# Layer 3's last stage: sixteen scatters spread over the dense steps, and seven more dense steps ahead of the slot experts

## The chip, the core and the metric

The kernel runs on one core of one Trainium2 chip, as one launch. The metric is device time in microseconds (us), lower is better; the number quoted is the median of the runs. The core has five engines that run side by side and meet only through semaphores: TensorE (matmuls, PE in the profile, with PEld its weight loads), VectorE (DVE), ScalarE (ACT), GpSimd (POOL) and SyncE (SP, which only issues transfers). GpSimd also issues transfers here, among them all indirect ones (scatters).

## What is computed

A decoder of four layers on x of 4 batches x 512 tokens x 128 channels. Each layer adds self-attention, cross-attention to a context of 77 rows, and a feed-forward block. Only the end of layer 3 matters here: the last batches of cross-attention, and the mixture of experts behind it:

```python
logits = (X @ gate_w.T).astype(jnp.float32)
scores = jax.nn.sigmoid(logits)
_, idx = jax.lax.top_k(scores + bias[None, :], K)          # K = 4 of E = 32
w = jnp.take_along_axis(scores, idx, axis=-1)
w = w / jnp.clip(jnp.sum(w, axis=-1, keepdims=True), 1e-12, None)
...
pos = jnp.take_along_axis(jnp.cumsum(onehot, axis=0) - 1, eid[:, None], axis=1)[:, 0]
valid = pos < C                                            # C = 128 rows an expert
xe = jnp.zeros((E, C, D), x.dtype).at[eid, posc].add(jnp.where(valid[:, None], Xrep, ...))
h = jax.nn.silu(jnp.einsum('ecd,edi->eci', xe, W1)) * jnp.einsum('ecd,edi->eci', xe, W3)
ye = jnp.einsum('eci,eid->ecd', h, W2)
out = yrows.reshape(-1, K, D).sum(axis=1)
out = out + jax.nn.silu(X @ sw1.T) * (X @ sw3.T) @ sw2.T
```

Each of 2048 tokens goes to four of 32 experts, each expert takes at most 128 rows, in the order of the tokens, and a shared expert sees every token.

## The kernel before

The kernel does this mixture in two ways. Batches 0, 1 and 2 are *routed by slots*: each token's row is scattered to its places in a table `slots` in DRAM (32 experts x 128 places, 130 numbers a place: the row, its weight, and where it came from). The experts then run over the table, and each resulting row is scattered to a table `back`, from which four rows a token are fetched and added. Batch 3, whose places can only be known last, is done *densely*: all 16 pairs of experts and the shared expert run over its 512 tokens, and the routing weights (zero where an expert wasn't chosen) multiply the inner result.

The code is written as Python generators that `weave` (L391) advances against one another; a `yield` ends a step. The order so written is the order of priority for a scheduler, which sets the final order on each engine, except where `tc.manual_schedule(engines=...)` fixes an engine's order as written.

The parts, in the order of the program:

- Cross-attention of layer 3 (`l3_xattn`, L2200 on), 64 steps of lagged phases, woven with `chain5(b)` for b = 0, 1, 2: `route_slots` (L750) chooses experts and places, builds `sent` (the rows with weight and origin) and appends 16 scatters to `self.puts` (L789; 128 rows each). `put(n)` (L795) takes scatters off that list and issues them on GpSimd; `scores` of the cross-attention calls it with 2, in the last batch with 3, after each group. At its end `net.put(len(net.puts))` (L2455) issues whatever is left: the sixteen scatters of batch 2.
- Weights. Six packs of layer 3's experts lie in DRAM as bf16. `load` (L371, the issue at L376) fetches each twice: as f32, a transfer with a cast, issued by GpSimd (for the down-projections of batch 3 and all of the slots), and as bf16 unchanged, issued by SyncE (for batch 3's gate and up). The last three f32 packs and four of the bf16 packs go to memory that the cross-attention frees.
- `shared_rows` (L912), two steps for each of batches 0 to 2: the shared expert, whose result is added to x.
- `norm(3)`, `tokens_in_three` (L718), `route_dense` (L730): batch 3's normalised tokens as three bf16 parts, its routing, and the weights' transpose `w3T`. This is `chain`, one step of it being taken for each 0.3 steps of the work it is woven with.
- `ffn("l3_ffn", (3,), ...)` (L968), called `dense`: 17 steps, one for each pair of experts and the shared expert. A step has six bf16 matmuls (gate and up in three parts each), a silu on ScalarE (L1029) into `h` (five buffers), a product by up on VectorE and one by the weights that `spread3` brings out of `w3T`, and, two steps later, one f32 down-matmul into `acc` (L1037).
- `slot_experts` (L830): `fetch` (L842) loads the table in eight groups of four 128-row pieces, over SyncE; for each group `turn` (four transposes, L847), `inner` (gate and up), `inner_turn` (L871) and `down`, which scales the rows by their weights (`made`, L887 and L888) and issues four scatters to `back` (L890) on GpSimd, 32 in all.
- `returned` (L929): three fetches of 1 MB from `back` (L936), four adds a batch to x on VectorE, and the store. `net.out(3)` adds batch 3's dense result and stores it.

The order of these at the end, with the numbers the change touches:

```python
net.weave(chained(*shared, some(dense, 3)), chain, 0.3)
net.weave(net.slot_experts(at["l3"], ff), some(dense, 7), 4, 1)
with tc.manual_schedule(engines={mybir.EngineType.DVE}):
    back = net.returned(range(3), ff)
    next(back)
    net.weave(dense, back, 0.2, 6)
```

So three dense steps stand ahead of the slot experts, seven are woven into them (one for every four slot steps), and seven follow, with the returned rows' adds behind the sixth.

Of the kernel before, what the change touches and what calls it, by code (L numbers as in the profile page):

```python
# [13 lines left out]
F32 = mybir.dt.float32  # L14
# [277 lines left out]
class Net:  # L292
# [361 lines left out]
    def spread(self, w, group, away, pool):  # L654

        nc = self.nc
        T, E = w.shape[1], w.shape[2]
        wp = pool.tile([P, T, E], F32, name="w_halves", tag="w_halves", bufs=1)
        nc.gpsimd.tensor_copy(
            wp.rearrange("p t (h u) -> p t h u", h=2), w.rearrange("p t (u h) -> p t h u", h=2)  # L660
        )
        yield
        for i, b in enumerate(group):
            t = self.sm((E, S))
            for j in range(TB):
                nc.tensor.transpose(t[:, j * P : j * P + P], wp[:, TB * i + j, :], self.ident)
            wT = pool.tile([E, S], F32, tag="w_turned", name="w_turned", bufs=2)
            self.move(wT, t)
            nc.sync.dma_start(away[b], wT)
            yield  # L670
# [124 lines left out]
    def put(self, n):  # L795

        for _ in range(min(n, len(self.puts))):
            self.puts.pop(0)()

    def alone(self, group, put):  # L800

        self.tc.declare_no_dep(put.ins, group=group, reason="rows of their own")
        self.tc.add_to_no_dep_group(group, put.ins)
# [108 lines left out]
    def shared_rows(self, b, W, pool):  # L912

        nc = self.nc
        H = D // 2
        pg, pu = (self.bank("f", (P, S)) for _ in range(2))
        self.dot(pg[:H], (W["gs0"][:, :H], self.tokens(b)))
        self.dot(pu[:H], (W["us0"][:, :H], self.tokens(b)))
        h = pool.tile([P, S], F32, tag="h", name="h", bufs=5)
        nc.scalar.activation(h[:H], pg[:H], AF.Silu)  # L920
        self.tt(h[:H], h[:H], pu[:H], ALU.mult)
        yield
        ps = self.bank("f", (P, TB, D))
        for j in range(TB):
            self.dot(ps[:, j, :], (h[:H, j * P : j * P + P], W["ds0"][:H]))
        self.add_rows(b, ps)
        yield
# [40 lines left out]
    def ffn(self, stage, group, E, base, pool, spread=None):  # L968

        nc = self.nc
        packs = self.units_of(stage, group)
        blocks = [packs[i : i + 2] for i in range(0, len(packs), 2)]
        away = self.chunks[stage] if not spread else None
        rest = [(b, [int(u) for u in routed]) for blk in blocks for b in group for _, _, routed in blk if routed]
        coming = []

        def chunk():  # L980

            if not rest or spread:
                return
            b, units = rest.pop(0)
            c = pool.tile([P, UNITS, S], F32, tag="c", name="c", bufs=3)
            for h in range(2):
                first = h * E // 2 + units[0]
                src = away[b, first : first + len(units)].rearrange("e s -> (e s)")
                nc.sync.dma_start(
                    c[64 * h : 64 * h + 64, : len(units)].rearrange("p e s -> p (e s)"), src.partition_broadcast(64)  # L990
                )
            coming.append(c)

        y = {b: pool.tile([P, S], F32, tag="y", name="y", bufs=2 * len(group)) for b in group}
        self.sums.update({(stage, b): y[b] for b in group})
        chunk()
        chunk()
        at = base
        for k, blk in enumerate(blocks):
            Ws = [self.pack(at + i, n) for i, (n, _, _) in enumerate(blk)]  # L1000
            names = {W: n for W, (n, _, _) in zip(Ws, blk)}
            at += len(blk)
            ahead = at + len(blocks[k + 1]) - 1 if k + 1 < len(blocks) else at + 1
            for b in group:
                units = [(W, u, None) for W, (_, sh, _) in zip(Ws, blk) for u in sh]
                plan = []
                for W, (_, sh, routed) in zip(Ws, blk):
                    plan += [(W, u, None) for u in sh] + [(W, u, i) for i, u in enumerate(routed)]
                acc, cs = {}, {}
                for i, (W, u, in_c) in enumerate(plan):  # L1010
                    if in_c is not None and spread:
                        if u not in cs:
                            cs.update(spread([v for _, v, in_c in plan[i : i + 2] if in_c is not None]))
                        cu = cs.pop(u)
                    elif in_c is not None:
                        if in_c == 0:
                            chunk()
                            c = coming.pop(0)
                        cu = c[:, in_c, :]
                    pg, up = self.bank("f", (P, S)), self.bank("f", (P, S))  # L1020
                    for ps, w in ((pg, "g"), (up, "u")):
                        if spread:

                            wb = self.in_bf16[names[W]][w + u]
                            self.dot(ps, *[(wb, self.x3[:, i]) for i in range(3)])
                        else:
                            self.dot(ps, (W[w + u], self.tokens(b)))
                    h = pool.tile([P, S], F32, tag="h", name="h", bufs=5)
                    nc.scalar.activation(h, pg, AF.Silu)  # L1029
                    self.tt(h, h, up, ALU.mult)  # L1030
                    if in_c is not None:
                        self.tt(h, h, cu, ALU.mult)

                    def down(W=W, u=u, h=h, i=i, b=b, acc=acc, n=len(plan), k=k):
                        if i == 0:
                            acc["t"] = self.acc()
                        nc.tensor.matmul(acc["t"], lhsT=W["d" + u], rhs=h, start=i == 0, stop=i == n - 1)  # L1037
                        if i == n - 1 and k == 0:
                            nc.scalar.copy(y[b], acc["t"])
                        elif i == n - 1:  # L1040
                            self.tt(y[b], y[b], acc["t"], ALU.add)

                    self.last.append(down)
                    if len(self.last) > 2:
                        self.last.pop(0)()
                    if b == group[0] and i == 2:
                        self.want(ahead)
                    yield
# [1231 lines left out]
def chained(*chains):  # L2280
    for c in chains:
        yield from c


def some(steps, n):

    for _ in range(n):
        if next(steps, steps) is steps:
            return
        yield  # L2290


def build(nc, packs, dram):
# [9 lines left out]
    at = {}  # L2303
# [6 lines left out]
    with tile.TileContext(nc) as tc, ExitStack() as ctx:  # L2310
        net = Net(ctx, tc, packs, dram, feed)
# [3 lines left out]
        def open_pool(name, right=False):  # L2315
            pools[name] = ExitStack()
            return pools[name].enter_context(net.pool(name, right=right))
# [29 lines left out]
        ff = open_pool("ff")  # L2347
# [60 lines left out]
        dense = lambda b: net.l2_dense(b, y[b], w4, s4)  # L2408
# [26 lines left out]
        steps = net.l3_xattn(at["x3"], x3)  # L2435
# [14 lines left out]
        with tc.manual_schedule(engines={mybir.EngineType.Pool}):  # L2450
            net.weave(some(steps, 32), chain5(0), 1.7)
            net.want(at["l3"] + 1)
            net.weave(some(steps, 32), chain5(1), 1.7)
            net.weave(steps, chain5(2), 1.2)
            net.put(len(net.puts))  # L2455
        net.add_columns(3, net.sums.pop(("l3_xattn", 3)))
        close_pool("x3")
        close_pool("x3c")
# [2 lines left out]
        ff = open_pool("ff3")  # L2461
# [5 lines left out]
        shared = [net.shared_rows(b, net.stay[of("l3_ffn")[0]], ff) for b in range(3)]  # L2467
        chain = chained(net.norm(3), net.tokens_in_three(3, ff), net.route_dense(3, W5, s5))

        dense = net.ffn("l3_ffn", (3,), 32, at["l3"], ff, net.spread3)  # L2470
        net.weave(chained(*shared, some(dense, 3)), chain, 0.3)
        net.weave(net.slot_experts(at["l3"], ff), some(dense, 7), 4, 1)
        with tc.manual_schedule(engines={mybir.EngineType.DVE}):
            back = net.returned(range(3), ff)
            next(back)
# [26 lines left out]
```

## Time and profile before

| | us |
|---|---|
| median of 3 runs | 2211.4 (2210.07 to 2212.25) |
| the profiled execution | 2231.3 |
| its span in the profile | 2229.6 |

How to read it: times in the profile count from the start of the span, and the profiled execution's own time is 1.7 us more than its span. A row of a timeline gives start, duration, engine, line, operation, written<-read tiles, how many, and in brackets how long the engine had been idle and who ended that. A row of the chain of waits gives start, length, and the engine and line that the end of the program depended on in that time.

The end of the program, by stretch (busy us of TensorE, VectorE, ScalarE and GpSimd, and the granted TensorE clock):

| stretch, us | what runs | TensorE | VectorE | ScalarE | GpSimd | clock |
|---|---|---|---|---|---|---|
| 2110 to 2128 | shared expert, batch 2's scatters | 8.23 | 5.34 | 4.70 | 14.03 | 0.82 |
| 2128 to 2141 | batch 3's routing, slot fetches, f32 weights | 11.38 | 6.38 | 5.15 | 0.37 | 0.63 |
| 2141 to 2149 | three dense steps | 7.78 | 4.78 | 2.37 | 0.00 | 0.72 |
| 2149 to 2156.5 | first slot groups, dense | 7.45 | 3.05 | 3.16 | 0.01 | 1.00 |
| 2156.5 to 2204.5 | slot groups, dense, rows returned | 37.90 | 20.24 | 15.33 | 31.24 | 0.93 |
| 2204.5 to 2217 | the last dense steps, fetch of returned rows | 12.47 | 8.27 | 2.98 | 0.00 | 1.00 |
| 2217 to 2229.6 | adds and stores | 1.61 | 8.91 | 0.00 | 0.00 | 0.64 |

A busy engine need not be at its peak: matmul records overlap, and their ends are modelled.

### The profile page before, as it was taken

To read this page: it belongs to the slowest core of one execution; us is meant where nothing else is said; L and a number is where in the kernel's file an instruction comes from. 1 tells how busy PE (TensorE), PEld (TensorE's weight loads), DVE (VectorE), ACT (ScalarE), POOL (GpSimd) and SP (SyncE) were. 2 spreads that over 40 slices of the span, in tenths; PEclk is the share of its full clock that TensorE was granted. 3 is DMA by queue.
4 is the path that set the end of the run, shared out by engine and by line. 5 is a ranking of instruction groups with operands and counts; after the bars stand their busy time and mean duration, and the time that the engine had idled before them with its cause. 6 is when DMAs were issued, how large, how long until landed. Compare 5 with 4: busy or idle time off the path is not lost.

```text
span 2229.6 us, 28185 instructions
## 1 busy us (share of the span) xinstructions
PE 2085.8 (94%) x8982; PEld 1106.7 (50%) x8988; DVE 1602.6 (72%) x4045; ACT 1012.1 (45%) x2052; POOL 567.1 (25%) x705
## 2 busy tenths in 40 slices
PE   6999899999999999899999999999999999499886
PEld 3556546645544554445444544444444455276543
DVE  6677575566675769778977788777777866589745
ACT  4565445542434554444543444434434434456532
POOL 1000010000000000433333333333333332535733
PEclk8999899999999999999999999999999999799978
DMA  6321135154444343333443344444554444121122
GB/s 170 94 72 45 47 103 133 55 136 113 108 131 100 91 116 85 98 86 103 106 115 99 103 121 121 119 129 112 133 140 125 126 121 133 26 96 34 31 74 78
DMA packets 92116, 224.37 MB, mean 101 GB/s; under 512 B 22227, under 2 KB 41107, under 8 KB 91711
## 3 DMA queue, kind: packets, MB, share of 16 engines
q1 hardware_dynamic: 88398, 218.63, 37.2%
q0 software_dynamic: 3568, 3.93, 0.6%
q8 instruction: 71, 1.16, 0.2%
q14 instruction: 79, 0.64, 0.1%
HBM read 193.43 MB, written 23.53 MB: 97 GB/s over the span
## 4 chain that ended last, share of the span: by engine, by line
PE 71%; DVE 18%; ACT 5%; issue 2%; POOL 1%; DMA 1%; another core or an unknown queue 1%; SPq 0%; DVEq 0%; ACTq 0%; POOLq 0%
PE mm L426 19%; PE f L426 13%; PE s L426 8%; PE mm L1878 7%; PE acc L1037 6%; PE mm L1850 4%; PE mm L1825 4%; DVE h L437 2%; PE mm L1227 1%; DVE m L1167 1%; DVE at_m L1911 1%; PE mm L1205 1%; PE mm L1160 1%; DVE gvx L437 1%; DVE x L437 1%
## 5 line engine op out<-in xcount | busy, mean ns | idle before, releaser
L1786 POOL TENSOR_TENSOR gvx<-gvx 128x512 f32<-128x512 f32 (+1 forms) x256 | 260.7, 1018 | 548.5 <-DVE gvx L437 470.3
L426 PE MATMUL f<-xT,w_l_ffn 128*128 128x512 f32 (+1 forms) x700 | 338.7, 606 | 1.2 <-ACT h L1029 0.7
L1913 ACT ACTIVATE at_e<-mm,at_m 128x512 f32<-128x512 f32 x256 | 173.1, 686 | 265.8 <-DVE at_m L1911 260.4
L426 PE MATMUL mm<-w_l_ffn_qkv,xT 128*128 128x512 f32 x512 | 265.5, 605 | 5.0 <-ACT at_e L1913 2.2
L1878 PE MATMUL mm<-og,w_l_ffn_o 128*128 128x512 f32 x512 | 263.6, 600 | 2.0 <-DVE og L437 1.9
L437 DVE TENSOR_TENSOR h<-h,f 128x512 f32<-128x512 f32 (+1 forms) x192 | 131.3, 685 | 151.9 <-PE f L426 109.7
L1029 ACT ACTIVATE h<-f 128x512 f32<-128x512 f32 x189 | 112.4, 596 | 248.1 <-PE f L426 205.3
L1037 PE MATMUL acc<-h,w_l_ffn 128*128 128x512 f32 x378 | 197.3, 607 | 3.5 <-DVE h L437 2.9
L437 DVE TENSOR_TENSOR gvx<-mm,gv 128x512 f32<-128x512 f32 x256 | 174.3, 684 | 27.5 <-PE mm L426 23.4
L426 PEld LDWEIGHTS f<-xT,w_l_ffn 128*128 128x128 f32 (+1 forms) x700 | 127.1, 192 | 133.5 <-issue 112.6
L437 DVE TENSOR_TENSOR og<-mm,c 128x512 f32<-128x512 f32 x256 | 173.8, 682 | 25.6 <-PE mm L1878 23.7
L1826 ACT COPY eT<-mm 128x512 f32<-128x512 f32 x256 | 137.4, 596 | 77.5 <-PE mm L1825 77.3
L1911 DVE TENSOR_REDUCE at_m<-mm 128x1 f32<-128x512 f32 x256 | 161.4, 682 | 14.4 <-PE mm L426 13.6
L1825 PEld LDWEIGHTS mm<-ident,at_e 128*128 128x128 f32 x1024 | 119.7, 141 | 66.6 <-issue 44.9
L1878 PEld LDWEIGHTS mm<-og,w_l_ffn_o 128*128 128x128 f32 x512 | 90.6, 190 | 110.8 <-issue 86.1
L1825 PE MATMUL mm<-ident,at_e 128*128 128x128 f32 x1024 | 134.8, 274 | 4.1 <-ACT at_e L1913 4.1
L426 PEld LDWEIGHTS mm<-w_l_ffn_qkv,xT 128*128 128x128 f32 x512 | 87.3, 190 | 96.6 <-issue 58.8
L426 PE MATMUL mm<-roped 64*128 64x512 f32 x512 | 130.8, 622 | 1.6 <-DVE roped L437 1.3
L1167 DVE TENSOR_REDUCE m<-mm 128x1 f32<-128x512 f32 (+3 forms) x176 | 104.9, 636 | 31.8 <-PE mm L1163 30.8
L1850 PE MATMUL mm<-eT,v 128*64 128x512 f32 x512 | 117.0, 598 | 0.0
L1037 PEld LDWEIGHTS acc<-h,w_l_ffn 128*128 128x128 f32 x378 | 72.2, 196 | 88.9 <-issue 62.0
L437 DVE TENSOR_TENSOR h<-h,c 128x512 f32<-128x512 f32 x160 | 111.6, 703 | 4.0 <-DMA c<-l_ffn_w 1.1
(503 smaller groups left out, 3552.6 us busy)
## 6 DMA issues: line engine op xcount, KB each, us to landing
c<-gates SPq DMA_DIRECT2D x256, 256.0 KB
c<-l_ffn_w SPq DMA_DIRECT2D x96, 384.0 KB
w_l_ffn_qkv<-in_l_ffn_qkv SPq DMA_DIRECT2D x24, 640.0 KB
w_l_ffn<-in_l_ffn SPq DMA_DIRECT2D x26, 576.0 KB
w_l_ffn_o<-in_l_ffn_o SPq DMA_DIRECT2D x24, 512.0 KB
rot<-qk SPq DMA_DIRECT2D x128, 64.0 KB
d<-inverted SPq DMA_DIRECT2D x64, 128.0 KB
k_parts<-k SPq DMA_DIRECT2D x12, 384.0 KB
```

Of the source, the lines that this page charges most:

```text
L426: self.nc.tensor.matmul(out, lhsT=lhsT, rhs=rhs, start=i == 0, stop=i == len(pairs) - 1)
L437: self.nc.vector.tensor_tensor(out, a, b, op)
L1029: nc.scalar.activation(h, pg, AF.Silu)
L1037: nc.tensor.matmul(acc["t"], lhsT=W["d" + u], rhs=h, start=i == 0, stop=i == n - 1)
L1167: nc.vector.tensor_reduce(m[:, i, h0 : h0 + per], ps, AX.X, ALU.max, negate=True)
L1786: nc.gpsimd.tensor_tensor(x[:, :, :m], x[:, :, :m], x[:, :, m : 2 * m], ALU.add)
L1825: nc.tensor.transpose(p[:, j, :], es[i][hl][:, j * P : j * P + P], self.ident)
L1826: nc.scalar.copy(eT[hl][:, :, i * P : i * P + P], p)
L1850: nc.tensor.matmul(po[64 * hl : 64 * hl + 64, :], lhsT=m["v"][:, j, hl, :], rhs=eT[hl][:, j, :], start=j == 0, stop=j == TB - 1,)
L1878: nc.tensor.matmul(acc, lhsT=W["o"][:, (e - 1) * D : e * D], rhs=hs.pop(e - 1), start=e == 1, stop=e == E)
L1911: nc.vector.tensor_reduce(m, s, AX.X, ALU.max, negate=True)
L1913: nc.scalar.activation(e[:, :n], s, AF.Exp, bias=m, accum_out=den)
```

## The change

It does four things. The sixteen scatters of batch 2 are no longer issued at the end of the cross-attention. A new generator `paced` goes around the shared and dense steps: after each step it has GpSimd copy one column of the newest `h` to a small tile `seen`, and then issues one scatter, all on GpSimd in the written order; so each scatter stands behind a copy that waits for that `h`. Ten dense steps instead of three stand ahead of the slot experts, and four instead of seven are woven into them, one for every six slot steps instead of four; three are left for the end instead of seven. And since the scatters have moved, GpSimd's three late f32 weight loads stand ahead of them in its queue.

```diff
+    def paced(self, steps, pool):
+
+        for step in steps:
+            yield
+            if self.puts:
+                seen = pool.tile([64, 1], F32, tag="seen", name="seen", bufs=2)
+                self.nc.gpsimd.tensor_copy(seen, self.newest)
+                self.put(1)
...
         self.tt(h[:H], h[:H], pu[:H], ALU.mult)
+        self.newest = h[:H, :1]
...
                     self.tt(h, h, up, ALU.mult)
+                    self.newest = h[:64, :1]
...
             net.weave(steps, chain5(2), 1.2)
-            net.put(len(net.puts))
...
-        net.weave(chained(*shared, some(dense, 3)), chain, 0.3)
-        net.weave(net.slot_experts(at["l3"], ff), some(dense, 7), 4, 1)
+        with tc.manual_schedule(engines={mybir.EngineType.Pool}):
+            net.weave(net.paced(chained(*shared, some(dense, 10)), ff), chain, 0.3)
+            net.put(len(net.puts))
+        net.weave(net.slot_experts(at["l3"], ff), some(dense, 4), 6, 1)
```

On GpSimd the order of the changed program is: the last scatters of batch 1, the three f32 weight loads, then sixteen pairs of `seen` and scatter (two pairs for each of the three shared `h`, one for each of the ten dense ones, with the clearing of batch 3's `sb` after the second pair), then the 32 scatters to `back`. On TensorE the order is the same as before up to the third dense step. SyncE's queue keeps its order.

## The prediction

> **What bounds the end now.** I read the page first, for span and totals; then the chain of waits over the last 380 us; then the timelines of GpSimd (POOL) and of SyncE's queue (SPq) around the edit; then ScalarE's timeline, for the pace of a dense step. The edit touches only what comes after 2100 us of this page:
> ```profile
> span 2229.6 us, 28185 instructions
> PE 2085.8 (94%) x8982; PEld 1106.7 (50%) x8988; DVE 1602.6 (72%) x4045; ACT 1012.1 (45%) x2052; POOL 567.1 (25%) x705
> ```
> The chain of waits (start, length, what) of that end has five steps whose releaser the profile does not know:
> ```profile
> 2118.35 6.72 another core or an unknown queue
> 2125.68 2.95 another core or an unknown queue
> ...
> 2164.17 2.43 another core or an unknown queue
> ...
> 2180.73 3.62 another core or an unknown queue
> ...
> 2195.45 4.28 another core or an unknown queue
> ```
> They sum to 20.0 us. In each, matmuls have run by their records, and TensorE's semaphore comes microseconds later (a gate matmul modelled to end at 2119.98 releases ScalarE at 2125.07). The profiled execution took 2231.3 us, the median of the runs shown is 2211.4: 19.9 more. The likeliest reading is that these late results belong to the profiled execution.
>
> Now GpSimd's queue (start, length, what):
> ```profile
> 2104.39 1.35 POOL L789 DMA_INDIRECT slots<-sent,to  x1 [0.15 <-issue]
> ...
> 2125.70 0.97 POOL L789 DMA_INDIRECT slots<-sent,to  x1 [0.30 <-issue]
> 2126.67 1.71 POOL L376 DMA_DIRECT2D w_l_ffn<-in_l_ffn  x3
> 2156.49 1.04 POOL L890 DMA_INDIRECT back<-made,slots  x1 [28.11 <-ACT made L887]
> 2157.84 1.01 POOL L890 DMA_INDIRECT back<-made,slots  x1 [0.30 <-issue]
> ...
> 2203.50 0.97 POOL L890 DMA_INDIRECT back<-made,slots  x1 [0.30 <-issue]
> ```
> and SyncE's:
> ```profile
> 2127.85 8.61 SPq L842 DMA_DIRECT2D slots<-slots  x8
> 2205.66 1.46 SPq L936 DMA_DIRECT2D back<-back  x3
> ```
> The reader sees one string of work. Batch 2's scatters end at 2126.67; the slot fetches leave 2.15 us after the last scatter's start; the first fetch has landed at 2134.74; TensorE turns the first slots at 2148.68, after three dense steps; the first row goes back at 2156.49. From there 32 scatters of 1.28 us (0.97 and a gap of 0.30) need at least 31 x 1.28 + 0.97 = 40.7 us; they take 48.0, to 2204.47. The returned rows are fetched at 2205.66, land at 2211.1, 2213.8 and 2216.4, but their adds begin at 2216.70, behind the last dense steps on VectorE, and the program ends at 2229.6: 25.1 us after the last scatter.
>
> Without its late results this end fits the median. GpSimd's string would be 2156.5 - 9.7 + 40.7, plus a tail of 18.4 (below): 2205.9, and with the 1.7 us outside the span 2207.6. TensorE's own line sets the rest, to 2211.4. So the two are within 4 us of each other, and lengthening GpSimd's string shows nearly in full.
>
> **The change, part by part.** The pace of a dense step:
> ```profile
> 2202.32 0.60 ACT L1029 ACTIVATE h<-f 128x512 f32<-128x512 f32 x1 [2.67 <-issue]
> ...
> 2214.65 0.60 ACT L1029 ACTIVATE h<-f 128x512 f32<-128x512 f32 x1 [1.56 <-DVE h L437]
> ```
> Six starts, five steps in 12.33 us: 2.47 us a step.
>
> *Seven more dense steps ahead of the slots.* The instruction order of the changed program is the same on TensorE up to the third dense step; then come seven more where the first slot turn stood: 7 x 2.47 = 17.3 us. All ten down-matmuls now stand ahead of the turn, of which one did before; seven lie in the steps, two more cost 2 x 0.86 = 1.7. The steps are moved, not added; what they free later is counted below.
>
> *Scatters paced.* Each of the sixteen now follows a small copy (`seen`) that waits for a step's `h`; the last waits for dense step 10. No row shows a 64x1 copy: nearest are the 128x32 memset (0.15 us) and the 128x308 product (0.7); I take 0.2, with the gap 0.4. Sixteen pairs of some 1.5 us fit into steps of 2.47, so fifteen are hidden by the dense work; without that cover each pair would cost its 1.5. Only the last is on the path. Counted from the last up-matmul: 1.5 to `h` (two 0.69 products), 0.4, 2.15 from scatter to fetch, and the fetch. The fetch took 6.9 beside three weight loads; alone I estimate 3.6, since a returned batch of 1 MB landed 5.5 after its issue, of which 2.6 is moving at 400 GB/s, and the slot fetches landed 0.9 apart. Sum 7.7, less three down-matmuls that TensorE still has (2.6): it stands still for 5.1 us. Before, this latency was covered, with 14 us to spare (2134.74 to 2148.68). The Trainium skill, DMA: Bandwidth & Descriptors, "Anatomy of one DMA - SWDGE (gpsimd) path", prices a DMA at about 2.0 us plus its bytes at 436 GB/s. By that, scatter and fetch are 4.6 (estimate) where I have 5.75, and the stall 4.0. I keep the trace's; ends 3.5 and 7.
>
> Queued behind the `seen` waits: the memset of `sb` for batch 3's router, after two pairs, so at about 2120 for a use at 2133.85 (hidden), and the silu of the fifth step on, whose `h` buffer waits for GpSimd's copy (five buffers, 12 us, hidden). The three weight loads go ahead, to about 2106, beside SyncE's four at 2110-2112; those landed by 2116 and would land some 4 us later, for a use after 2133: nothing.
>
> *From first turn to first returned row.* 7.8 us now, of which some 3.4 is dense work between. Without it the chain is turn 0.6, copy 0.65, inner 0.95, silu and product 0.9, turn and copy 0.8, down and scale 1.6: 5.5. The skill's TensorE: Matmul & The Clock Gate, Part 1, speaks against the change: after some 3.4 us idle TensorE runs at half clock until it has been busy as long. The row agrees in kind: granted clock 0.63 in 2128-2141, after the idle before it, and nine bf16 matmuls took 3.69 us there against some 2 later. By the rule a 5.1 us stall costs up to 1.7, without it nothing; I take 1.0. Net -1.3.
>
> *Slot stage.* Four dense steps beside eight groups in place of seven: TensorE has about 2.4 us a group and 1.2 of dense, against GpSimd's 5.1. So GpSimd runs through: 48.0 becomes 40.7, -7.3 (bounds -7.3 and 0).
>
> *Tail.* Three dense steps remain (7.4 us, and some 5 of closing), ended by the first landing 6.65 after the last scatter. The adds then start on landing: 6.65 + 12 x 0.70 + 3.3 from last add to end = 18.4, for 25.1: -6.7.
>
> Sum on the profiled execution: 17.3 + 1.7 + 5.1 - 1.3 - 7.3 - 6.7 = +8.8. To timed runs: the old chain loses 19.9. The new chain contains only the first two late steps (9.7); the others fall into TensorE's slack beside GpSimd. So 2231.3 + 8.8 - 9.7 = 2230.4: **2230 us**, 0.84% slower.
>
> **Rivals.** (1) *The late results are in timed runs too*, and the 19.9 us lie spread elsewhere. Then only +8.8: 2220. For it: they sit in semaphores, which ScalarE really obeyed. Against: with the first two in place GpSimd's string alone gives 2156.5 + 40.7 + 18.4 + 1.7 = 2217.3, over the 2211.4 measured.
> (2) *Bursts of scatters cause the late results*, in timed runs too: the first falls inside the run of sixteen, and pacing removes its 9.7. Then 8.8 - 9.7 = -0.9: 2210.5, no change. Against: twos and threes of scatters from 2043 to 2104 show none.
> (3) *Faster:* as (2), and the hand-over is at its short ends too: stall 3.5 (-1.6), no clock loss (-1.0), dense steps at TensorE's 2.37 (-0.7), first returned row after 5.0 (-0.5), giving 2206.7. It decides only if more than 8.8 + 4.4 = 13.2 us vanish from the hand-over and the late results together.
> That the pacing does nothing is excluded: every `seen` waits for its own `h` in the program.
>
> **How the numbers follow.** 0.2% is 4.4 us, about what a measurement of this kernel can tell from no change. Main case 0.68 (2225 to 2237: stall and clock at their ends, waits in the slot stage returning); rival 1, 0.20 (2215 to 2224); rival 2, 0.07; rival 3, 0.05. The range takes the first two: 2215 to 2237. Slower 0.88, same 0.07, faster 0.05.
>
> **What would show it.** Right: the first slot turn some 22 to 24 us later from the end of the cross attention; a TensorE gap of about 5 us before it that ends on the slot fetch; 32 returning scatters with 0.30 gaps, 41 us; adds that begin when the rows land. Wrong: a first turn within 10 us of the old one, or GpSimd waiting in the slot stage as before. The forecast fails if late results were never the profile's own.

## The result and the profile after

The changed kernel takes 2233.5 us (median of 4 runs, 2230.7 to 2241.5); beside it the kernel before takes 2211.7 (4 runs). The ratio is 1.010, 95% interval 1.0069 to 1.0131: slower by some 22 us. The forecast was 2230.

The profiled execution of the changed kernel took 2235.9 us, 1.7 more than its span. The page's head:
```profile
span 2234.2 us, 28223 instructions
PE 2086.8 (93%) x8988; PEld 1107.1 (50%) x8988; DVE 1602.7 (72%) x4045; ACT 1012.3 (45%) x2052; POOL 570.3 (26%) x721
```
TensorE has the work of before (8988 weight loads in both; 2085.8 us busy then); GpSimd has 3.2 us more, the sixteen copies. So the time is in the order of the work, not in its amount. Unlike before, the chain of waits (the work that the end of the program depended on) has no step with an unknown releaser; where it has such steps, this text calls them *late results*. Its pieces at the hand-over and at the end (start, length, what):
```profile
2161.72 2.12 DMA slots<-sent,to
2163.86 0.03 issue
2163.89 2.96 DMA slots<-slots
2166.85 0.14 issue
2166.99 1.10 PE f L856 x4
...
2214.86 2.11 DMA back<-made,slots
2216.99 0.03 issue
2217.02 5.42 DMA back<-back
2222.47 0.70 DVE x L437
```
The end waits for the last paced scatter, for the fetch of the slots behind it, then for the slot stage, then for the last scatter to `back` and its fetch. Line numbers have moved by nine to eleven: the slot turn is L856, the scatter to `back` L899.

TensorE's timeline shows the hole that the hand-over leaves (start, length, engine, line, what; in brackets the idle time before and who ended it):
```profile
2157.57 1.46 PE L426 MATMUL f<-x,w_l_ffn 128*128 128x512 bf16 x6
2158.86 2.86 PE L1048 MATMUL acc<-h,w_l_ffn 128*128 128x512 f32 x6
2166.99 1.09 PE L856 MATMUL f<-ident,slots 128*128 128x128 f32 x4 [5.26 <-DMA slots<-slots]
```
Ten dense steps are done and TensorE stands still for 5.26 us until the slots land. Before, three dense steps ran ahead of the turn, and the slots had landed 14 us before it.

GpSimd's timeline: the weight loads now stand first, a copy and a scatter follow each step, and the 32 scatters to `back` run without holes.
```profile
2107.96 1.70 POOL L376 DMA_DIRECT2D w_l_ffn<-in_l_ffn  x3
2118.13 0.18 POOL L806 COPY seen<-h 64x1 f32<-64x1 f32 x1 [8.47 <-DVE nmr L490]
2118.88 1.05 POOL L789 DMA_INDIRECT slots<-sent,to  x1 [0.57 <-issue]
...
2160.97 0.18 POOL L806 COPY seen<-h 64x1 f32<-64x1 f32 x1 [1.18 <-DVE h L437]
2161.72 0.97 POOL L789 DMA_INDIRECT slots<-sent,to  x1 [0.57 <-issue]
2175.30 0.97 POOL L899 DMA_INDIRECT back<-made,slots  x1 [12.61 <-ACT made L896]
2176.57 0.97 POOL L899 DMA_INDIRECT back<-made,slots  x1 [0.30 <-issue]
...
2214.86 0.97 POOL L899 DMA_INDIRECT back<-made,slots  x1 [0.30 <-issue]
```
Counted from the end of the cross-attention the last scatter to `slots` starts at 49.8, before at 15.4. And VectorE ends on the landing of the returned rows, with nothing else in its way:
```profile
2222.47 8.44 DVE L437 TENSOR_TENSOR x<-x,back 128x512 f32<-128x512 f32 x12 [11.55 <-DMA back<-back]
```

Where profiles are set side by side below, times count from the end of the cross-attention (ScalarE's copy `yT`, at 2111.92 in this profile). The 2100 us ahead of it are the same in all kernels, but that point itself falls between 2108 and 2123 from one execution to the next; the stretch behind it, the *end stage*, is the cleaner measure.

### The profile page after: what moved, and what is told of

Same layout as the page of the kernel before. It is cut to its first block, busy times and chain, and to the rows that moved or that the text cites. A ratio compares the mean times of both kernels' runs of the same rounds, so it can differ in the third digit from the quotient of the medians.

```text
span 2234.2 us, 28223 instructions
## 1 busy us (share of the span) xinstructions
PE 2086.8 (93%) x8988; PEld 1107.1 (50%) x8988; DVE 1602.7 (72%) x4045; ACT 1012.3 (45%) x2052; POOL 570.3 (26%) x721
## 5 line engine op out<-in xcount | busy, mean ns | idle before, releaser
L1922 DVE TENSOR_REDUCE at_m<-mm 128x1 f32<-128x512 f32 x256 | 161.5, 683 | 14.4 <-PE mm L426 13.5
L1836 PEld LDWEIGHTS mm<-ident,at_e 128*128 128x128 f32 x1024 | 119.3, 141 | 66.6 <-issue 45.4
```

The lines of the kernel that those rows point to most:

```text
L1836: nc.tensor.transpose(p[:, j, :], es[i][hl][:, j * P : j * P + P], self.ident)
L1922: nc.vector.tensor_reduce(m, s, AX.X, ALU.max, negate=True)
```

## The experiments

The table has every profile; each column is told in us. "Turn" is the first slot turn and "row" the first scatter to `back`, both from the end of the cross-attention; "scatters" is from the start of the first of the 32 to the end of the last; "tail" from there to the end of the span; "late" is the sum of the steps of the chain of waits whose releaser is unknown.

| kernel | turn | row | scatters | tail | end stage | late | timed, against before |
|---|---|---|---|---|---|---|---|
| before, first profile | 38.4 | 46.2 | 48.0 | 25.1 | 119.3 | 20.0 | |
| again (before) | 31.0 | 38.8 | 40.6 | 19.8 | 99.2 | 0 | |
| the changed kernel | 55.1 | 63.4 | 40.5 | 18.4 | 122.3 | 0 | 1.0100 (1.0069 to 1.0131) |
| dense_only | 48.0 | 54.2 | 40.7 | 18.6 | 113.5 | 0 | 1.0056 (1.0037 to 1.0076) |
| paced_only | 43.5 | 53.7 | 40.5 | 19.8 | 114.0 | 0 | 1.0063 (1.0039 to 1.0087) |
| loads_first | 29.2 | 37.0 | 40.5 | 19.9 | 97.5 | 0 | 0.9986 (0.9965 to 1.0007) |
| two_a_step | 47.8 | 54.0 | 40.6 | 18.4 | 113.0 | 0 | 1.0074 (1.0047 to 1.0101) |
| six_ahead | 36.7 | 44.2 | 40.6 | 20.0 | 104.8 | 0 | 1.0032 (1.0011 to 1.0052) |
| none_ahead | 23.9 | 34.1 | 40.5 | 25.4 | 100.1 | 0 | 1.0007 (0.9991 to 1.0022) |
| none_woven | 22.9 | 32.3 | 42.8 | 21.5 | 96.7 | 0 | 1.0001 (0.9982 to 1.0020) |
| after_2 | 55.0 | 63.3 | 47.4 | 18.5 | 129.2 | 11.3 | 1.0062 (1.0042 to 1.0083) |
| two_a_step_2 | 48.6 | 54.7 | 48.3 | 18.5 | 121.5 | 7.7 | 1.0013 (0.9991 to 1.0036) |
| dense_only_2 | 53.9 | 60.1 | 49.2 | 18.6 | 127.9 | 9.6 | 1.0058 (1.0036 to 1.0081) |
| late_woven | 24.0 | 33.1 | 51.4 | 31.7 | 116.2 | 5.1 | 0.9995 (0.9974 to 1.0016) |

Three sets ran on three chips, with the kernel before timed in each (median of its runs in brackets): again, dense_only, paced_only and loads_first (2214.6, median of 14 runs), two_a_step to none_woven (2211.2, 29 runs), after_2 to late_woven (2227.9, 35 runs).

**again** is the kernel before, unchanged, profiled a second time.

> The kernel before, unchanged, looked at once more for its late TensorE results. If the five waits without a known releaser (20.0 us in its first profile) belong to that one profiled execution, this profile has none over 2 us, a span near 2210 us and one time near 2211. If they come from bursts of scatters, they stand here again at about the same places and the span is near 2230.

2214.6 us, span 2212.9, no late result. TensorE turns the first slots, GpSimd's 32 scatters take 40.6 us, and the adds begin when the rows land:
```profile
2144.68 0.60 PE L847 MATMUL f<-ident,slots 128*128 128x128 f32 x4
```
```profile
2152.49 1.04 POOL L890 DMA_INDIRECT back<-made,slots  x1 [20.21 <-ACT made L887]
...
2192.16 0.97 POOL L890 DMA_INDIRECT back<-made,slots  x1 [0.30 <-issue]
```
```profile
2194.32 1.46 SPq L936 DMA_DIRECT2D back<-back  x3
```
```profile
2199.94 1.42 DVE L437 TENSOR_TENSOR x<-x,back 128x512 f32<-128x512 f32 x2 [1.61 <-DMA back<-back]
```
SyncE issues the fetch at 2194.32, VectorE adds from 2199.94: 5.62 later, as in the changed kernel (5.45). The fetch follows the start of the last scatter by 2.16 or 2.17 us in every profile here, so the scatters set it (the chain of waits of this profile names a silu of ScalarE that ended at about the same time). So the 48.0 us of the slot stage and the adds queued behind dense steps, from which I took gains, were effects of the late results in one profile: with the same program and none of them, neither is there. On this chip rival 1 falls, since an execution without late results takes the median time, and so does rival 2, since both bursts of scatters are in this profile.

**dense_only** keeps the scatters in a row, as before, and makes the change of the dense steps alone:

```diff
-        net.weave(chained(*shared, some(dense, 3)), chain, 0.3)
-        net.weave(net.slot_experts(at["l3"], ff), some(dense, 7), 4, 1)
+        net.weave(chained(*shared, some(dense, 10)), chain, 0.3)
+        net.weave(net.slot_experts(at["l3"], ff), some(dense, 4), 6, 1)
```

> One part of the change alone: ten dense steps ahead of the slots and four beside them, the sixteen scatters issued in a row as before. My theory: the dense steps ahead cost 17.3 + 1.7 on GpSimd's string, the wait of about 5 us for the slot fetch is gone, and so is the half clock after it (some 2 us); with a first returned row some 2 us sooner after the first turn the end is at about 2225 us, 13 over before and 8 under the changed kernel. If it is the pacing that costs, this one stays within 4 us of 2211.7.

2226.0 us.
```profile
2159.55 0.60 PE L847 MATMUL f<-ident,slots 128*128 128x128 f32 x4
```
The first turn comes 17.0 us later than in again (48.0 for 31.0); with nothing dense in between, a turn now leads to its first row in 6.2 us, not 7.8.

**paced_only** keeps three dense steps ahead and seven woven, and paces the scatters:

```diff
...
-            net.put(len(net.puts))
...
-        net.weave(chained(*shared, some(dense, 3)), chain, 0.3)
+        with tc.manual_schedule(engines={mybir.EngineType.Pool}):
+            net.weave(net.paced(chained(*shared, some(dense, 3)), ff), chain, 0.3)
+            net.put(len(net.puts))
+        net.weave(net.slot_experts(at["l3"], ff), some(dense, 7), 4, 1)
```

> The other part alone: scatters one a step behind the weight loads, with three dense steps ahead of the slots and seven beside them as before. Nine of the sixteen find a step or its end, the other seven go in a row behind the third dense step. My theory: the last scatter leaves about 9 us after that step's h, the fetch 2.15 later, the data 3 later: the first slot turn comes some 14 us later than in the kernel before, with TensorE standing still for most of it, so about 2224 to 2227 us. If pacing costs nothing and the dense steps ahead are all of it: 2211.7 within 4 us.

2227.3 us. With only nine steps to stand behind, nine of the sixteen scatters are paced and the rest come in a row behind the last. TensorE's timeline:
```profile
2148.50 1.88 PE L1048 MATMUL acc<-h,w_l_ffn 128*128 128x512 f32 x4
2163.90 1.12 PE L856 MATMUL f<-ident,slots 128*128 128x128 f32 x4 [13.52 <-DMA slots<-slots]
```
It waits 13.52 us for the slots. So each part alone costs 11 to 13 us by the medians, and together they cost 22; by the end stage it is 14.3 and 14.8 for the parts and 23.1 for both. The ten dense steps cover part of the wait that the pacing makes.

**loads_first** makes only the last of the four edits, without pacing; the f32 weight loads then stand ahead of twelve of the sixteen scatters (in the changed kernel, of all):

```diff
-            net.put(len(net.puts))
...
+        with tc.manual_schedule(engines={mybir.EngineType.Pool}):
+            net.put(len(net.puts))
         net.weave(chained(*shared, some(dense, 3)), chain, 0.3)
```

> Only the order on GpSimd's queue: the three weight loads stand ahead of twelve of the sixteen scatters of batch 2, no pacing, dense steps three and seven as before. My theory: scatters end 1.7 us later, the slot fetch lands alone and so some 4 us sooner after its issue, and neither is what ends a wait: 2211.7 within 3 us. If the loads ahead of the scatters push the bf16 loads or the slots onto the path: some 4 us slower.

2209.8 us, no difference that can be told. The loads cost nothing, as forecast.

**two_a_step** is the changed kernel with two scatters behind each copy, so that the last waits for the second dense step and not the tenth:

```diff
-                self.put(1)
+                self.put(2)
```

> The changed kernel with two scatters behind each copy in place of one, so that the last of the sixteen waits for the second dense step and not for the tenth; ten dense steps still stand ahead of the slots. If the waiting for the last scatter and the half clock behind it are what the pacing costs (7.1 us later first turn, 2.1 us longer to the first returned row), they vanish and the time is that of ten dense steps ahead alone: 2225 to 2227 us, with no idle TensorE before the first slot turn. If the copies and the spread scatters cost something by themselves (GpSimd's port, transfers in small pieces), it stays near 2233.

The profile shows what was expected. TensorE no longer waits for the slots:
```profile
2169.68 1.02 PE L1048 MATMUL acc<-h,w_l_ffn 128*128 128x512 f32 x2
2170.54 0.60 PE L856 MATMUL f<-ident,slots 128*128 128x128 f32 x4
```
The turn follows the tenth step without a gap, a row goes back after 6.2 us, and the end stage is 113.0 us, as in dense_only (113.5) and 9.3 below the changed kernel. The median, 2232.2, missed the 2225 to 2227: six runs lie at 2222.8 and 2223.0 and from 2231 to 2237, and the profiled one (2237.5) had lost its time before the change begins, its cross-attention ending 11 us later than the changed kernel's. So it was run again, below.

**six_ahead**, **none_ahead** and **none_woven** start from loads_first and change how many dense steps stand ahead of the slots (6, 0, 0), how many are woven in (7, 7, 10) and, with it, behind which of the remaining steps the adds begin. The last of them:

```diff
-        net.weave(chained(*shared, some(dense, 3)), chain, 0.3)
-        net.weave(net.slot_experts(at["l3"], ff), some(dense, 7), 4, 1)
+        net.weave(chained(*shared, some(dense, 0)), chain, 0.3)
+        net.weave(net.slot_experts(at["l3"], ff), some(dense, 10), 3, 1)
...
-            net.weave(dense, back, 0.2, 6)
+            net.weave(dense, back, 0.5, 5)
```

> Weight loads ahead of the scatters, no pacing, six dense steps ahead of the slots (three in the kernel before, ten in the changed one), seven woven, four left. If each dense step ahead of the slots lengthens GpSimd's string by its own 2.47 us: three more than in the kernel with the loads first (2209.8), so 2217 us. If TensorE's own line were the bound, the order of its steps would matter little: 2210 to 2212.

> Weight loads ahead of the scatters, no pacing, no dense step ahead of the slots, seven woven, ten left, the returned rows' adds behind the ninth of them. The slots' data lands about 23 us after the cross-attention and the routing of batch 3 ends on TensorE at about 22, so the first turn comes 5 us sooner (24 instead of 29.2). If GpSimd's string were still the bound to the end: 2205. But ten dense steps now lie behind the slot stage, so I expect the adds to wait for VectorE's dense products: the last silu about where it was, the first add some 2 to 4 us after the rows have landed, and 2207 to 2211, no gain that counts.

> As the kernel with none ahead, but ten dense steps woven into the slot experts (one for three slot steps), seven left, and the returned rows' adds taken two at a time behind the fifth of these seven. The slot stage must hold ten dense steps beside eight groups: 24.7 + 19.2 = 43.9 us of TensorE against 40.6 of GpSimd, so it may grow by 1 to 3 us. First turn 5 us sooner, adds in between the last dense products: 2204 to 2207, 0.2 to 0.3% under the kernel before. If TensorE's line bounds: 2208 to 2211.

2217.7, 2214.5 and 2212.7 us, where before takes 2211.2. Three more steps ahead lengthen the end stage by 7.3 us against loads_first, 2.43 a step, as the first theory said. Three fewer shorten nothing. In none_ahead the first turn comes 5.3 us sooner, but VectorE's timeline ends like this:
```profile
2202.85 0.69 DVE L437 TENSOR_TENSOR h<-h,f 128x512 f32<-128x512 f32 x1 [0.74 <-PE f L426]
2203.57 0.69 DVE L437 TENSOR_TENSOR h<-h,s 128x512 f32<-128x512 f32 x1
2204.18 1.41 DVE L437 TENSOR_TENSOR x<-x,back 128x512 f32<-128x512 f32 x2
```
The adds stand behind the last dense products, 11.3 us after the fetch was issued. In none_woven the dense work stretches the way from turn to row to 9.4 us and the slot stage to 42.8. The 2204 to 2207 of the first theory did not come. The times fit the second, that TensorE's own line bounds, but do not isolate it: VectorE's fixed order holds the adds back too, and the profiles differ in the clock (20.5 us at half clock behind the cross-attention in none_ahead, 13.7 in none_woven, 10.2 in loads_first and six_ahead).

**after_2**, **two_a_step_2** and **dense_only_2** are the changed kernel, two_a_step and dense_only once more, side by side. **late_woven** is none_woven with its dense steps later: eight woven in, the first behind the first returned rows, and nine left.

```diff
+        net.weave(chained(*shared, some(dense, 0)), chain, 0.3)
+        net.weave(net.slot_experts(at["l3"], ff), some(dense, 8), 3.5, 3.5)
...
+            net.weave(dense, back, 0.5, 7)
```

> The changed kernel once more, so that it stands on the same chip as the two below. By the first measurement 2233.5 us (1.0% over before); from the end of the cross-attention to the end of the span 122 us in the profile.

> Two scatters behind each copy, once more. In its first profile the wait before the first slot turn was gone and the end stage took 113.0 us as with ten dense steps ahead alone (113.6; the changed kernel 122.3), but its cross-attention ended 11 us later than the changed kernel's, and its median was 2232. If that lateness was chance, it now takes 9 us less than the changed kernel beside it and the same as ten dense steps alone: 2224 to 2227. If something of the pacing slows the timed runs, it stays within 3 us of the changed kernel.

> Ten dense steps ahead of the slots, no pacing, once more beside the two above: 2225 to 2227 us, end stage 113.6 us in the profile. If two scatters a copy cure the hand-over, the two are equal within 3 us; if pacing itself costs, this one is 6 us or more faster.

> Weight loads ahead of the scatters, no pacing, no dense step ahead of the slots; eight dense steps woven into the slot experts, the first only behind the first returned rows, and nine left, with the returned rows' adds two at a time behind the seventh of these. In the kernel with none ahead and ten woven the dense work between stretched the way from first turn to first returned row to 9.4 us and the slot stage to 42.8. If GpSimd's string still bounds: first turn at 23 us after the cross-attention, 6.2 to the first returned row, 40.6 of scatters, an end stage of 91 to 94 us in place of 96.7, and 2203 to 2207. If TensorE's own line bounds (its last silu came 80.7 us after the cross-attention with the loads first, 82.5 with ten woven): 95 to 98 us, and 2208 to 2212, no gain.

This chip turned out to be another case: the kernel before took 2227.9 us on it, 13 to 17 more than on the other two, and all four profiles have late TensorE results, for 5 to 11 us of their chains; no profile of the kernel before was taken on it. They took 2241.4, 2232.2, 2243.3 and 2225.9 us.

The cure of the hand-over shows in the times here: two_a_step_2 is 9.2 us faster than after_2, as expected, and 7.7 in the end stage. But it is not equal to dense_only_2, which I expected: it is 11 us faster. TensorE's timelines of the same piece of work, first of dense_only_2, then of two_a_step_2:
```profile
2140.07 2.07 PE L426 MATMUL f<-w_l_ffn,h 64*128 64x128 f32 x8 [1.77 <-DVE h L437]
2142.07 3.67 PE L426 MATMUL f<-xT,w_l_ffn 128*64 128x512 f32 x4
```
```profile
2121.21 1.16 PE L426 MATMUL f<-w_l_ffn,h 64*128 64x128 f32 x8
2122.29 1.93 PE L426 MATMUL f<-xT,w_l_ffn 128*64 128x512 f32 x4
```
The same twelve matmuls take 5.7 us in one and 3.0 in the other. In dense_only_2 (its profiled execution, 2253.0 us, is the slowest of its twelve) the granted clock was at half for 27.3 us on end (2130.3 to 2157.6), in two_a_step_2 for three stretches of 3.4 between 2115 and 2140; its first turn came 5.3 us sooner. That the sixteen scatters in a row bring on such half clock is not shown: 13.7 us on end stand in again, which has them in a row, and in the changed kernel and two_a_step, which pace them. Nor is it shown that the clock is the whole of the 11 us between the medians, of which these two profiles show 6.4 in the end stage.

late_woven measures the same as before. Its TensorE stops for 3.85 us in the slot stage while VectorE and ScalarE wait for results that its records show as done:
```profile
2160.82 0.38 PE L871 MATMUL f<-ident,inner 128*128 128x128 f32 x2
2165.06 1.16 PE L426 MATMUL f<-w_l_ffn,slotsT 128*128 128x128 f32 x7 [3.85 <-ACT slotsT L849]
```
Its scatters took 51.4 us, and the adds, which stand behind dense products on VectorE, came 16.3 after the fetch was issued. So it can't say what its order gives where no late results come; that stays open. No order tried beats the kernel before by a measurable amount.

## Why the prediction was right, and which of its terms were not

The forecast of the sign and of the cost holds: the two parts put work and a wait on the string of GpSimd and the slots, which sets the end. Its two gains do not: they belonged to the late results of one profile. The time, 2233.5, is 3.5 over 2230 and within the range. Step by step, against again, since neither that profile nor the changed kernel's has late results:

*Seven dense steps ahead and the hand-over.* Forecast: the first turn 17.3 + 1.7 + 5.1 = 24.1 later. Measured: 55.07 - 31.00 = 24.07. Of this the steps are 17.0 (dense_only), and the hand-over with the two down-matmuls 7.1, where I had 6.8. Again, the changed kernel and two_a_step (47.8) have the same stretches at half clock ahead of the turn, 13.65 and 3.41 us, so these three compare cleanly: 16.8 for the steps and 7.3 for the hand-over. That the sum agrees to 0.1 us is luck; loads_first, with 10.2 us at half clock, has its turn 1.8 sooner than again. TensorE's idle time was 5.26 for 5.1. The wait came out right although its pieces did not, which is luck too: the fetch landed 2.96 us after its issue, not 3.6, while copy and gap ahead of the scatter took 0.75, not 0.4. The price of a transfer by the Trainium skill (DMA: Bandwidth & Descriptors, "Anatomy of one DMA - SWDGE (gpsimd) path") made scatter and fetch 4.6 and the wait 4.0; the trace has 5.13 (2.17 and 2.96) and 5.26. That section is about transfers that GpSimd issues, and the fetch is SyncE's, so the trace does not test it for the fetch.

*From first turn to first row.* Forecast -1.3, measured 8.31 - 7.81 = +0.5: this term failed. The part without the wait was right (dense_only: 6.22, so -1.6). What I under-priced is the half clock behind the wait: 8.31 - 6.22 = 2.1 us, for 1.0. The changed kernel by stretches (length; busy time of TensorE, its weight loads, VectorE, ScalarE and GpSimd with their instructions; granted clock; share of the DMA engines and GB/s):
```profile
2162.00:2167.00 5.00, 0.01 (x1) 0.04 (x1) 0.00 (x0) 0.00 (x0) 0.69 (x1) 0.95 0.42 104
2167.00:2169.00 2.00, 1.32 (x5) 0.93 (x6) 0.00 (x0) 0.59 (x1) 0.00 (x0) 0.50 1.06 279
2169.00:2171.00 2.00, 2.00 (x10) 2.00 (x11) 0.00 (x0) 0.14 (x1) 0.00 (x0) 0.50 1.20 307
2171.00:2173.00 2.00, 1.92 (x9) 1.21 (x8) 0.85 (x2) 0.83 (x2) 0.00 (x0) 0.50 0.90 218
2173.00:2175.00 2.00, 2.00 (x17) 1.53 (x17) 0.56 (x2) 0.72 (x3) 0.00 (x0) 0.91 0.01 2
```
TensorE's clock was at half for 6.8 us (2166.6 to 2173.4), twice the time that the Trainium skill, TensorE: Matmul & The Clock Gate, Part 1, gives for warming up. By its rule the cost was at most 1.7 (estimate); at half clock for 6.8 us it is at most half of that, 3.4, and 2.1 was measured. Without the wait, in dense_only and two_a_step, the clock stayed at 1.00 there. The first slot turn and its copy leave TensorE idle again (1.32 of 2.00 us busy), but that this is why one busy stretch was not enough is not shown: in again TensorE was busy for all of the 13.3 us from 2120.9 to 2134.2, by its records, at a granted clock of 0.50. (The prediction's nine bf16 matmuls of 3.69 us ran at 2142.34, not in 2128 to 2141; the clock was at half there as well.)

*Slot stage.* Forecast -7.3, measured -0.1 against again. The step said that fewer dense steps beside the slots let GpSimd run through. GpSimd runs through with seven too (40.64); and with four it takes 47.4 when late results come (after_2). The 48.0 belonged to the late results and not to the dense steps.

*Tail.* Forecast -6.7, measured 18.4 - 19.8 = -1.4, for the same reason: without late results the adds begin on landing before the change too.

*From the profile to the timed runs.* The forecast took three sums off the first profile: 9.7 for late results, and 7.3 and 6.7 as gains of the change, 23.7 in all. Between the two profiles of the kernel before, the end stages differ by 20.1 (119.3 and 99.2), all of it late results, and the real gains are 0.1 and 1.4: 21.6. So I took off 2.1 too much, and the first profile had reached the end of the cross-attention 3.4 sooner than again: I was 5.5 too low here and 1.8 at the first row. The number stands near the measured one because the late results were taken off once, under whatever name, and not because the gains were there. By these terms the profiled execution should have taken 2237.7. It took 2235.9, as its cross-attention ended 1.8 sooner than in again, and the median is 2.4 lower still, in runs that spread by 10 us. That these 4.2 us lie on the forecast's side is luck.

*TensorE's own line.* The prediction said that GpSimd's string alone gives 2207.6 and TensorE sets the rest. That was wrong: in again the chain of GpSimd, slots and returned rows reaches to the end (first row at 2152.49, then 40.64 and 19.8: 2212.9). My string was 7 us short, because I had taken the whole 9.7 off where the first turn lay only 7.4 later, had the tail at 18.4, and the cross-attention ended 3.4 sooner in the first profile. But a second string is near: none_ahead and none_woven gain 5.3 and 6.3 us on the first turn against loads_first (29.2), and nothing that counts at the end. Whether that string is TensorE's, or VectorE's with its fixed order, these runs do not separate.

*The rivals.* Rival 1, late results in timed runs too, fits the third chip, where all four profiles have them: the forecast there was +8.8, measured is +13.5 (9.4 to 18.5 by the interval). With four dense steps beside them the scatters took 47.4 us there, not the 40.7 that this forecast contained. Rival 2, that bursts of scatters cause late results, is not settled: in the five profiles that have them, nearly all fall while GpSimd issues scatters one behind another, and none in the dense steps between; but nine other profiles, which all have the burst of 32, have none. Rival 3 fell.

## What to carry to other kernels

Before a stall in a profile is turned into a gain, ask whether it belongs to the kernel or to that execution: a second profile of the unchanged kernel would have shown that 12.5 of 14 us of forecast gain were not there. A producer that is paced by its consumer's engine must finish early enough to hide its own latency, so the last item of a paced series costs its whole way (copy, scatter, fetch, warm-up), and two a step in place of one took that cost away here. And on a string that bounds the end, work moved ahead costs its own length, while work moved off it pays only down to the next string, here within 3 us (end stages of 99.2, 97.5 and 96.7).

## What the runs showed of the hardware

TensorE's results can come microseconds after its matmuls end by their records, in some executions: 20.0 us of one chain, 0 in the next profile of the same kernel, and 5 to 11 in all four profiles on one chip. The ends of matmuls are modelled. In late_woven TensorE was idle from 2161.2 to 2165.0 at a granted clock of 1.00, so it was not the clock. What holds them back is open.

The granted clock changes in steps of 3.41 us, the window that the Trainium skill, TensorE: Matmul & The Clock Gate, Part 1, gives (stretches of 3.41, 6.83, 10.24, 13.65 and 27.31 us at half in these profiles). Executions of one program differ by that: in batch 3's routing dense_only had 13.7 us at half clock, dense_only_2 27.3.

A 64x1 copy on GpSimd that had to wait for its `h` takes 0.18 us in the changed kernel, and the scatter behind it mostly starts 0.56 us after its end, where a scatter behind a scatter starts after 0.30. The first slot group lands 2.96 us after its issue there, with no weight loads beside it, and after 6.89 in the first profile of the kernel before, beside three of them.
